# Gated graph network and graph attention in one kernel: the attention weights of the last pair but one are transposed on TensorE

## The chip, the cores and the metric

The kernel runs on one core of a Trainium2 chip. The metric is the device time of one execution in microseconds (us). The profile is of one execution on the chip. Its engines are PE (TensorE, matmuls; PEld is its weight load), DVE (VectorE), ACT (ScalarE), POOL (GpSimd) and SP (SyncE, which only issues transfers).

## The reference

There are 64 graphs of 256 nodes with 256 features, and an adjacency matrix of integers for each. Two layers follow each other, each with a layer norm and a ReLU in front and a residual behind. The first is a gated graph network of three steps, the second a graph attention layer:

```python
# layer 0: three GRU steps
A = (adj != 0)
for i in range(3):
    m = h @ weight[i]
    aggr = einsum('bst,bsd->btd', A, m)
    gi, gh = aggr @ w_ih.T + b_ih, h @ w_hh.T + b_hh
    r, z = sigmoid(i_r + h_r), sigmoid(i_z + h_z)
    n = tanh(i_n + r * h_n)
    h = (1 - z) * n + z * h
# layer 1: attention
h = x @ W.T
e = leaky_relu((h @ a_left)[:, :, None] + (h @ a_right)[:, None, :])
e = where(adj == 0, -1e9, e)
out = softmax(e) @ h
```

All is float32.

## The kernel before

The 64 graphs are taken as 32 pairs (p = 0 to 31, G = 2 graphs g to a pair). A tile is 128 partitions by 512 float32: both graphs of a pair, or one graph as two blocks of 128 rows. Matmuls that need more than one rounded product use split operands: a float32 value is split into three tiles of the rounded type float32r (helper split, L469: part "0" on ACT at L472, "1" and "d" on DVE at L473 and L475). A projection is then a "top" of several matmuls into a PSUM bank (L497), a rescaling of that bank on ACT (L511, names with "scale"), and a "rest" (L502).

One pair goes through these stages:

- Input: norm and ReLU (norm_relu, L542), hi and lo parts for the propagation, and the transposed h, called hT.
- Three GRU layers (i = 0, 1, 2). Each splits hT ("h0", "h1"), multiplies by the adjacency ("prop 0", "prop 1", L618), splits the result ("g0", "g1"), and computes for both feature blocks db = 0, 1 the gates r, nh, ni and z. The top of r is cut in two: topT (the part of h) and topF (the part of the aggregate). ACT applies tanh (L637, L647, L650) and DVE combines (u, u add, d sub, d mul, d add: L642, L645, L654, L656, L658). At the end the new h is transposed back ("back 0", "back 1"), and either split again for the next layer or added to x ("res").
- Attention: "mid" norm and ReLU, four dots with the two halves of the attention vector (L715), the row of the right dots spread over all partitions ("right"), leaky ReLU on ACT (L741), masking (L744), row maximum (L746), exponentials with their sums (L752), then the transposition of the weights ("p turn", "p copy"), the weighted sum of the nodes ("mix", L769), the projection by W ("project", L778 or L792), and the scaled result added to x ("out", L797).

The last pair (p = 31) has its own form, so that its end is short: the third layer's gates are computed for each graph apart (names "... of 0" and "... of 1"), "back" and "right" and "p turn" are transposes on TensorE, and the attention goes by row blocks (L803 to L838, names such as "last mix 1 0"). In the last two pairs (p >= 30) the projection is one plain float32 matmul group after a copy of the mix ("mix copy", L788) instead of a split.

A transposition by DMA (dma_turn, L516) is this: one DMA transpose of the float32 tile seen as 16-bit halves, two gathers of 64 partitions each, and a copy on ACT (join, L533, its instruction at L535) that puts the halves together again. For the attention weights of pairs 0 to 30 it reads as

```python
dma_turn(f"p turn {g}", pm_[g], pT, [((rs, ALL), planes(rs), slice(None))])
join(f"p copy {g}", rs, pT)
```

with pm_ the masked exponentials and pT what mix reads.

The order of all work is made by a planner (class Plan) when the program is built. Each operation has an engine, an estimated occupation and latency, the buffers that it reads and writes, and a priority worked out backward from due times. The planner places the operations one by one, at each step the one that can start first, and of those the one of lowest priority value. The table LEAD moves the priority of single operations by so many nanoseconds; a name with "late " in front is that of pair 30, with "last " of pair 31, and with neither it holds for all pairs (a prefixed operation takes both leads). Up to four pairs are in flight, so PE works on the gates of one pair while another waits for its transfers. On each engine the instructions then run strictly in the order that the planner wrote.

Of the kernel before, what the change touches and what calls it, by code (L numbers as in the profile page):

```python
# [24 lines left out]


LEAD = {
    "w load": 17000, "w d": -3000, "in 0 eps": -2000, "in 0 relu": 71000, "in 1 stats": -3000, "in 1 relu": 57000,
    "h0 0": 3000, "prop 0": 4000, "g0 0": -24000, "g0 1": -19000, "prop 1": 30000, "g1 1": 23000, "r 0 topT": 2000,
    "ni 0 topF": -18000, "u add 0": 1000, "z 0 topF": -114000, "z 0 rest": 11000, "z 0": 55000, "d add 0": -14000,  # L30
    "r 1 topT": -55000, "nh 1 rest": 5000, "ni 1 topF": -23000, "z 1 topF": -162000, "z 1 scale": -94000,
    "z 1": 51000, "d sub 1": -3000, "d add 1": -14000, "back copy 1": -43000, "mask 0": -6000,
    "mid 1 stats": -52000, "max 1": -19000, "c0 0": 12000, "late h0 d": -6000, "late prop 0": 13000,
    "late g0 0": -52000, "late r 0 topT": -7000, "late nh 0 topF": -29000, "late r 1 topT": -8000,
    "late ni 1 topF": -30000, "late tanh 1": -20000, "last A": 11000, "last in 0 stats": 9000,
    "last in 0 eps": 1000, "last prop 1": 19000, "last g1 0": 12000, "last r 0 topT": -5000,
    "last r 0 rest": -45000, "last nh 1 rest": -3000, "last lo 0": -88000, "last back 1": -80000,
    "last ni 0 of 0 topF": 18000, "last nh 1 of 0 rest": -5000, "last ni 1 of 0 topF": 19000,
    "last r 0 of 1 topF": -19000, "last nh 0 of 1 topF": -34000, "last ni 0 of 1 topF": -37000,
}  # L40


# [164 lines left out]
def tile_gated_gnn_then_gat(  # L207
# [39 lines left out]
    nc = tc.nc  # L247
    P = 128
    B, N, D = x.shape
    L = weight.shape[0]  # L250
    NB = N // P
# [5 lines left out]
    NPAIR = B // G  # L257
# [16 lines left out]
    ALL = (0, 1)  # L274
    ONE = (0,)

    def parts(b):
        return b.t[:, :GN].rearrange("p (k d) -> p k d", k=2)
# [3 lines left out]
    def pe(name, n, fn, **kw):  # L282
        return plan.op(name, "PE", n, n + 220, fn, **kw)

    def act(name, n, fn, **kw):
        plan.op(name, "ACT", n, n + 170, fn, **kw)
# [14 lines left out]
    MM, TR, PROP, PASS = 432, 109, 120, 232  # L301
    A512, V512, S512, VP256, C512 = 475, 605, 660, 392, 522
# [6 lines left out]
    ident = const.tile([P, P], F32, name="ident")  # L309
# [206 lines left out]
    def dma_turn(name, src, t, gathers):  # L516

        view = lambda q, blocks: t.t.bitcast(U16).rearrange("p (k q n) -> p q k n", q=2, n=P)[:, q, blocks, :]
        plan.op(name, "SP", 1370, 3700, lambda: nc.sync.dma_start_transpose(
            t.t.bitcast(U16).rearrange("p (c n) -> p c n", n=P), src.t.bitcast(U16)), r=[(src, ALL)], w=[(t, ALL)])

        def gather(dst, blocks):
            for q in range(2):
                nc.sync.dma_start(dst(slice(64 * q, 64 * q + 64)), view(q, blocks))

        for region, dst, blocks in gathers:
            plan.op(name + " gather", "SP", 1320, 4800 if blocks == slice(None) else 3500, lambda dst=dst, blocks=blocks: gather(dst, blocks),  # L530
                    r=[(t, ALL)], w=[region])

    def join(name, src, dst, order="b j n"):  # L533

        act(name, 1065, lambda: nc.scalar.copy(  # L535
            dst.t.bitcast(U16).rearrange("p (j n b) -> p j n b", j=2, b=2),
            src.t.bitcast(U16).rearrange(f"p ({order}) -> p j n b", j=2, b=2)), r=[(src, ALL)], w=[(dst, ALL)])

    def planes(b):
        return lambda rows: b.t[rows].bitcast(U16).rearrange("p (b k n) -> p b k n", b=2, n=P)  # L540
# [27 lines left out]
    def pair(p):  # L568
# [5 lines left out]
        A = [Buf("round") for _ in range(G)]  # L574
        h = [Buf("full") for _ in range(G)]
        hi, lo = [Buf("round") for _ in range(G)], [Buf("round") for _ in range(G)]
        for g in range(G):
            dve2("A", 340, lambda g=g: nc.vector.tensor_scalar(A[g].t, ADJ[p][g].t, 0.0, None, op0=ALU.not_equal),
                r=[(ADJ[p][g], ALL)], w=[(A[g], ONE)])
# [3 lines left out]
                r=[(h[g], ALL), (hi[g], ONE)], w=[(lo[g], ONE)])  # L583
        hT = [Buf("full") for _ in range(DB)]
        if p > 0:
            rs = [Buf("full") for _ in range(DB)]
# [5 lines left out]
        for db in range(DB if p == 0 else 0):  # L592
            pt = Buf("bank")

            def turn(db=db, pt=pt):
                for g in range(G):
                    for nb in range(NB):
                        nc.tensor.transpose(pt.t[:, (g * NB + nb) * P : (g * NB + nb + 1) * P],
                                            parts(h[g])[:, nb, ts(db, P)], ident)
# [5 lines left out]
        for i in range(L):  # L605
            last = i == L - 1
# [23 lines left out]
            for part in [(0,), (1,)] if apart else [ALL]:  # L630
                cols, of = columns(part), " of %d" % part[0] if apart else ""
                for db in range(DB):
                    plan.due = 1000.0 * SLOT * (3 * p + 2 * i) + (8000.0 * part[0] if apart else 0)
                    d = hT[db]
                    pr = gate(f"r {db}{of}", db, [("hh", hs), (i, gs)], tops, True, part=part)
                    r_, z_, u = Buf("full"), Buf("full"), Buf("full")
                    act(f"r {db}{of}", fit(575, part), lambda b=r_, k=pr, db=db, cols=cols: nc.scalar.activation(  # L637
                        b.t[:, cols], k.t[:, cols], AF.Tanh, bias=b_rz[:, db : db + 1], scale=0.5),
                        r=[(pr, ONE), ("b_rz", ONE)], w=[(r_, ONE)])
# [12 lines left out]
                        r=[(pz, ONE), ("b_rz", ONE)], w=[(z_, ONE)])  # L652
# [10 lines left out]
            if not last:  # L663
                hi, lo = [Buf("round") for _ in range(DB)], [Buf("round") for _ in range(DB)]
            for g, db in [(g, db) for g in range(G) for db in range(DB)] if apart else []:
                hn = Buf("bank")

                def back(g=g, db=db, hn=hn):
# [6 lines left out]
                    r=[(hn, ALL)], w=[(XR[g], ALL)])  # L675
            for db in range(0 if apart else DB):
                hn = Buf("full" if away else "bank")
                if away:
                    rs = Buf("full")
# [77 lines left out]
        for g in range(G if far else 0):  # L757
            sm = sms[g]
            dve("recip", 70, lambda sm=sm: nc.vector.reciprocal(sm.t[:, 8 : 8 + NB], sm.t[:, 4 : 4 + NB]),
                r=[(sm, (1,))], w=[(sm, (2,))])  # L760
            pT, pg, pv = Buf("full"), Buf("bank"), Buf("bank")
            rs = Buf("full")
            dma_turn(f"p turn {g}", pm_[g], pT, [((rs, ALL), planes(rs), slice(None))])
            join(f"p copy {g}", rs, pT)

            def mix(g=g, pT=pT, pg=pg):
                for db in range(DB):
                    for jb in range(NB):
                        nc.tensor.matmul(pg.t[:, ts(db, N)], parts(hb[g])[:, jb, ts(db, P)],  # L769
                                         pT.t.rearrange("p (i j n) -> p i j n", j=NB, n=P)[:, :, jb, :], start=(jb == 0), stop=(jb == NB - 1))  # L770

            pe(f"mix {g}", 4 * MM, mix, r=[(pT, ALL), (hb[g], ALL)], w=[(pg, ONE)])
            if p < NPAIR - 2:
                cs = split(f"c{g}", pg, True)

                def project(js, first, cs=cs, pv=pv):
                    for n, (ib, db, j) in enumerate((ib, db, j) for ib in range(NB) for db in range(DB) for j in js):
                        nc.tensor.matmul(pv.t[:, ts(ib, D)], cs[j].t[:, db * N + ib * P : db * N + (ib + 1) * P],  # L778
                                         fac["W"][:, j, db, :], start=(first and n == 0), stop=True, skip_group_check=True)

                pe(f"project {g}", 8 * PROP, lambda project=project: project((0, 1), True),
                   r=[(cs[0], ONE), (cs[1], ONE), ("facW", ((0, 0), (1, 0)))], w=[(pv, ONE)])
                act(f"project {g} scale", A512, lambda pv=pv: nc.scalar.activation(pv.t, pv.t, AF.Copy, scale=SPLIT + 1.0), w=[(pv, ONE)])
                pe(f"project {g} rest", 4 * PROP, lambda project=project: project((2,), False),
                   r=[(cs[2], ONE), ("facW", ((0, 1), (1, 1)))], w=[(pv, ONE)])
            else:
                ag = Buf("full")
                act(f"mix copy {g}", A512, lambda ag=ag, pg=pg: nc.scalar.copy(ag.t, pg.t), r=[(pg, ONE)], w=[(ag, ALL)])  # L788

                def project_whole(ag=ag, pv=pv):  # L790
                    for ib, db in [(ib, db) for ib in range(NB) for db in range(DB)]:
                        nc.tensor.matmul(pv.t[:, ts(ib, D)], ag.t[:, db * N + ib * P : db * N + (ib + 1) * P], wT[:, db, :],  # L792
                                         start=(db == 0), stop=(db == DB - 1))

                pe(f"project {g}", 4 * MM, project_whole, r=[(ag, ALL), ("wT", ALL)], w=[(pv, ONE)])
            for nb in range(NB):
                dve(f"out {g}", VP256, lambda b=XR[g], nb=nb, pv=pv, sm=sm: nc.vector.scalar_tensor_tensor(  # L797
                    parts(b)[:, nb, :], pv.t[:, ts(nb, D)], sm.t[:, 8 + nb : 9 + nb], parts(b)[:, nb, :],
                    op0=ALU.mult, op1=ALU.add), r=[(pv, ONE), (sm, (2,))], w=[(XR[g], (nb,))])
            dma("store", 256, lambda g=g, b=XR[g]: nc.sync.dma_start(rows(out, G * p + g), parts(b)), r=[(XR[g], ALL)])  # L800


        for g, ib in [(g, ib) for g in range(G) for ib in range(NB)] if not far else []:  # L803
# [7 lines left out]
                r=[row], w=[total])  # L811
# [64 lines left out]
```

## Time and profile before

| | |
|---|---|
| median of 3 runs | 2075.97 us |
| lowest and highest | 2074.25 and 2076.62 us |
| span of the profiled execution | 2066.4 us |
| granted TensorE clock, mean | 0.998 |
| PE busy | 2045.3 us, 99% |
| ACT copies of the DMA transposes (L535) | 308 of 1165 ns, 358.9 us |
| DMA transposes | 308, 3.2 us from issue to landing (median) |
| gathers of 128 KB | 492, 3.6 us from issue to landing |

The page is of one execution; times in it are from the span's start. [...] neighbours overlap in the record: the distance from one start to the next is what PE spends. A line's "idle before" names what ended the wait. The granted clock is the share of full speed that TensorE was allowed.

### The profile page before, as it was taken

Reading aid. Unit: us, or ns where it says so; the run is one execution under the profiler, and the core shown is the slowest. Engines: PE = TensorE matmul, PEld = TensorE weight load, DVE = VectorE, ACT = ScalarE, POOL = GpSimd, SP = SyncE. Lnnn points to the kernel's source line nnn. Section 1 sums busy time; section 2 is a strip of 40 time slices with the busy share of each in tenths; the row PEclk is TensorE's granted clock in tenths of the full one; section 3 lists DMA queues with packets and bytes.
Section 4 is the critical chain, followed back from the end, with each engine's and each line's share of the span. In section 5 each row is a group of like instructions: output and inputs, shape, how many; then the busy total and the mean of one; then the engine's idle time right before and its main releaser. Section 6 shows DMA issues by size and latency. Waiting matters only on the chain.

```text
span 2066.4 us, 31380 instructions
## 1 busy us (share of the span) xinstructions
PE 2045.3 (99%) x9949; PEld 1692.7 (82%) x9949; DVE 1737.0 (84%) x3888; ACT 1761.8 (85%) x3047; POOL 157.8 (8%) x198
## 2 busy tenths in 40 slices
PE   8999999999999999999999999999999999999998
PEld 6888888888887888888888888888888888788887
DVE  7788888888888888888888888888888888888877
ACT  6788898888888888888888888888888888888876
POOL 1000000000000000000000000000000000000000
PEclk9999999999999999999999999999999999999999
DMA  4257787657776667866676766777766778666632
GB/s 129 55 108 122 128 142 108 116 106 139 132 125 104 117 121 130 141 109 113 110 136 129 125 115 117 111 133 140 112 115 118 121 128 142 104 118 108 118 72 57
DMA packets 742918, 241.52 MB, mean 117 GB/s; under 512 B 666704, under 2 KB 742752, under 8 KB 742752
## 3 DMA queue, kind: packets, MB, share of 16 engines
q1 hardware_dynamic: 742720, 239.51, 65.6%
q8 instruction: 78, 1.28, 0.3%
q14 instruction: 88, 0.72, 0.1%
q10 hardware_dynamic: 32, 0.01, 0.0%
HBM read 61.09 MB, written 16.84 MB: 38 GB/s over the span
## 4 chain that ended last, share of the span: by engine, by line
PE 85%; DMA 5%; DVE 5%; ACT 3%; issue 1%; SPq 0%; ACTq 0%; DVEq 0%
PE bank L497 45%; PE bank L502 23%; PE bank L618 8%; DMA full<-full 5%; PE bank L778 4%; PE bank L769 4%; DVE round L473 1%; ACT full L535 1%; PE bank L446 1%; DVE round L475 1%; ACT full L563 1%; ACT bank L511 1%; DVE full L656 0%; DVE full L744 0%; ACT full L637 0%
## 5 line engine op out<-in xcount | busy, mean ns | idle before, releaser
L497 PE MATMUL bank<-round,fac 128*128 128x512 f32 (+1 forms) x2328 | 617.2, 393 | 0.4
L497 PE MATMUL bank<-round,fac_hh 128*128 128x512 f32 (+1 forms) x2328 | 612.4, 395 | 0.0
L497 PEld LDWEIGHTS bank<-round,fac 128*128 128x128 f32 x2328 | 433.7, 188 | 105.3 <-DVE round L473 2.0
L497 PEld LDWEIGHTS bank<-round,fac_hh 128*128 128x128 f32 x2328 | 430.6, 188 | 96.4
L511 ACT ACTIVATE bank<-bank 128x512 f32<-128x512 f32 (+1 forms) x582 | 334.6, 577 | 95.8 <-PE bank L497 88.0
L535 ACT COPY full<-full 128x1024 uint16<-128x1024 uint16 x308 | 358.9, 1165 | 31.3 <-DMA full<-full 23.6
L502 PE MATMUL bank<-round,fac 128*128 128x512 f32 (+1 forms) x1164 | 356.8, 392 | 0.2 <-ACT bank L511 0.2
L502 PE MATMUL bank<-round,fac_hh 128*128 128x512 f32 (+1 forms) x1164 | 354.1, 394 | 0.0
L475 DVE SCALAR_TENSOR_TENSOR round<-round,round 128x512 fp32r<-128x512 f32 x444 | 304.8, 688 | 8.1
L502 PEld LDWEIGHTS bank<-round,fac 128*128 128x128 f32 x1164 | 215.1, 188 | 55.4 <-ACT bank L511 6.0
L557 POOL TENSOR_TENSOR small<-small,nhalf 128x2 f32<-128x2 f32 x128 | 123.8, 975 | 1687.2 <-DVE small L555 1611.4
L502 PEld LDWEIGHTS bank<-round,fac_hh 128*128 128x128 f32 x1164 | 206.1, 188 | 44.9 <-ACT bank L511 7.4
L618 PEld LDWEIGHTS bank<-round,round 128*128 128x128 f32 x1536 | 208.6, 190 | 14.4 <-DVE round L696 0.5
L473 DVE TENSOR_TENSOR round<-bank,round 128x512 fp32r<-128x512 f32 x252 | 172.8, 686 | 56.2 <-ACT round L472 53.3
L618 PE MATMUL bank<-round,round 128*128 128x256 f32 x1536 | 215.9, 284 | 0.3 <-DVE round L696 0.3
L642 DVE SCALAR_TENSOR_TENSOR full<-full,bank 128x512 f32<-128x512 f32 (+1 forms) x194 | 131.7, 679 | 56.4 <-ACT full L637 52.0
L647 ACT ACTIVATE full<-full,vec 128x512 f32<-128x512 f32 (+1 forms) x194 | 139.4, 719 | 40.4 <-DVE full L645 20.5
L650 ACT ACTIVATE full<-bank,b_rz 128x512 f32<-128x512 f32 (+1 forms) x194 | 132.8, 684 | 45.5 <-PE bank L502 43.9
L472 ACT ACTIVATE round<-bank 128x512 fp32r<-128x512 f32 x252 | 145.9, 592 | 28.5 <-PE bank L618 26.7
L656 DVE SCALAR_TENSOR_TENSOR full<-full,full 128x512 f32<-128x512 f32 (+1 forms) x194 | 130.4, 672 | 32.3 <-ACT full L650 32.1
L473 DVE TENSOR_TENSOR round<-full,round 128x512 fp32r<-128x512 f32 x192 | 130.9, 682 | 27.5 <-ACT round L472 24.2
L645 DVE TENSOR_TENSOR full<-full,bank 128x512 f32<-128x512 f32 (+1 forms) x194 | 131.1, 676 | 24.4 <-PE bank L502 17.4
(98 smaller groups left out, 2292.8 us busy)
## 6 DMA issues: line engine op xcount, KB each, us to landing
full<-full SPq DMA_DIRECT2D x492, 128.0 KB, 3.6
x<-in_x_dram SPq DMA_DIRECT2D x64, 256.0 KB, 3.0
adj<-in_adj_dram SPq DMA_DIRECT2D x64, 256.0 KB, 4.3
full<-in_x_dram SPq DMA_DIRECT2D x64, 256.0 KB, 3.1
full<-full SPq DMA_DIRECT2D x248, 64.0 KB, 2.5
out_dram<-full SPq DMA_DIRECT2D x62, 256.0 KB, 2.5
full<-line SPq DMA_DIRECT2D x62, 128.0 KB, 3.7
full<-full SPq DMA_TRANSPOSE x308, 3.2
```

The source lines that it names most:

```text
L472: act(name + " 0", A512 if bank else C512, lambda: nc.scalar.activation(v0.t, v.t, AF.Copy, scale=BELOW), r=[(v, ALL)], w=[(v0, ONE)])
L473: (dve if bank else dve2)(name + " 1", V512, lambda: nc.vector.tensor_sub(v1.t, v.t, v0.t.bitcast(F32)), r=[(v, ALL), (v0, ONE)], w=[(v1, ...
L475: dve2(name + " d", V512, lambda: nc.vector.scalar_tensor_tensor(vd.t, v1.t.bitcast(F32), -SPLIT, v0.t.bitcast(F32), op0=ALU.mult, op1=ALU ...
L497: nc.tensor.matmul(bank.t[:, cols], f(m, j, kb), b.t[:, cols], start=(first and n == 0), stop=True, skip_group_check=True)
L502: nc.tensor.matmul(bank.t[:, cols], f(m, 2, kb), s[kb][2].t[:, cols], start=False, stop=True, skip_group_check=True)
L511: act(name + " scale", fit(575 if "nh" in name else 515, part), lambda: nc.scalar.activation(bank.t[:, cols], bank.t[:, cols], AF.Identity ...
L535: act(name, 1065, lambda: nc.scalar.copy(dst.t.bitcast(U16).rearrange("p (j n b) -> p j n b", j=2, b=2), src.t.bitcast(U16).rearrange(f"p ...
L618: nc.tensor.matmul(pa.t[:, ts(g, N)], b, parts(A[g])[:, sb, :], start=(n == 0), stop=(n == len(terms) - 1))
L642: dve(f"u {db}{of}", fit(S512, part), lambda u=u, k=ph, b=r_, cols=cols: nc.vector.scalar_tensor_tensor(u.t[:, cols], b.t[:, cols], 1.0, k ...
L645: dve(f"u add {db}{of}", fit(V512, part), lambda u=u, k=pn, cols=cols: nc.vector.tensor_add(u.t[:, cols], u.t[:, cols], k.t[:, cols]), r=[ ...
L647: act(f"tanh {db}{of}", fit(615, part), lambda u=u, en=en, cols=cols: nc.scalar.activation(u.t[:, cols], u.t[:, cols], AF.Tanh, bias=b_i[: ...
L650: act(f"z {db}{of}", fit(575, part), lambda b=z_, k=pz, db=db, cols=cols: nc.scalar.activation(b.t[:, cols], k.t[:, cols], AF.Tanh, bias=b ...
```

## The change

For the last two pairs that take this path, p >= NPAIR - 2 (of which only p = 30 comes here, since pair 31 has its own form), the attention weights are transposed by four TensorE transposes into a PSUM bank, and one ACT copy of that bank takes the place of the re-interleaving copy. It is meant to take the latency of two DMA steps out of the way to pair 30's mix, close to the end of the program. The estimates given to the planner are four transposes (4 x TR) on PE and a bank copy (A512) on ACT. Together with it the table LEAD is another: the four entries "in 0 eps", "in 1 stats", "prop 0" and "r 0 topT", which hold for all pairs, are gone, and the 24 entries of "late" and "last" give way to nine others, so that the planner's order for the last pairs is another too.

```diff
 LEAD = {
-    "w load": 17000, "w d": -3000, "in 0 eps": -2000, "in 0 relu": 71000, "in 1 stats": -3000, "in 1 relu": 57000,
-    "h0 0": 3000, "prop 0": 4000, "g0 0": -24000, "g0 1": -19000, "prop 1": 30000, "g1 1": 23000, "r 0 topT": 2000,
...
-    "mid 1 stats": -52000, "max 1": -19000, "c0 0": 12000, "late h0 d": -6000, "late prop 0": 13000,
-    "late g0 0": -52000, "late r 0 topT": -7000, "late nh 0 topF": -29000, "late r 1 topT": -8000,
-    "late ni 1 topF": -30000, "late tanh 1": -20000, "last A": 11000, "last in 0 stats": 9000,
-    "last in 0 eps": 1000, "last prop 1": 19000, "last g1 0": 12000, "last r 0 topT": -5000,
-    "last r 0 rest": -45000, "last nh 1 rest": -3000, "last lo 0": -88000, "last back 1": -80000,
-    "last ni 0 of 0 topF": 18000, "last nh 1 of 0 rest": -5000, "last ni 1 of 0 topF": 19000,
-    "last r 0 of 1 topF": -19000, "last nh 0 of 1 topF": -34000, "last ni 0 of 1 topF": -37000,
+    "w load": 17000, "w d": -3000, "in 0 relu": 71000, "in 1 relu": 57000, "h0 0": 3000, "g0 0": -24000,
+    "g0 1": -19000, "prop 1": 30000, "g1 1": 23000, "ni 0 topF": -18000, "u add 0": 1000, "z 0 topF": -114000,
...
+    "late res 1": -12000, "late project 0": 6000, "last h0 d": -12000, "last r 0 topF": -52000,
+    "last nh 1 topF": 30000, "last ni 0 of 0 topF": 43000, "last ni 1 of 0 topF": 6000,
+    "last r 1 of 1 topT": -5000, "last z 1 of 1 topF": -9000,
 }
...
             pT, pg, pv = Buf("full"), Buf("bank"), Buf("bank")
-            rs = Buf("full")
-            dma_turn(f"p turn {g}", pm_[g], pT, [((rs, ALL), planes(rs), slice(None))])
-            join(f"p copy {g}", rs, pT)
+            if p < NPAIR - 2:
+                rs = Buf("full")
+                dma_turn(f"p turn {g}", pm_[g], pT, [((rs, ALL), planes(rs), slice(None))])
+                join(f"p copy {g}", rs, pT)
+            else:
+                pt = Buf("bank")
+
+                def turn(g=g, pt=pt):
+                    for k, (ib, jb) in enumerate((ib, jb) for ib in range(NB) for jb in range(NB)):
+                        nc.tensor.transpose(pt.t[:, ts(k, P)], parts(pm_[g])[:, ib, ts(jb, P)], ident)
+
+                pe(f"p turn {g}", 4 * TR, turn, r=[(pm_[g], ALL)], w=[(pt, ONE)])
+                act(f"p copy {g}", A512, lambda pt=pt, pT=pT: nc.scalar.copy(pT.t, pt.t), r=[(pt, ONE)], w=[(pT, ALL)])
```

In the order that the planner makes of this, PE has at the end of pair 31's third layer: the gates of graph 0, "late p turn 0", "late mix 0", "late project 0", "late p turn 1", "late mix 1", "late project 1", each with gates of graph 0 or 1 between, and then the last gates of graph 1 ("last r 1 of 1", "last z 1 of 1"). Before, all gates of both graphs stood ahead of "late mix 0".

## The prediction

> **What bounds the kernel now.** I read the page's first part, then the busy time by stage over the last 120 us, then TensorE's timeline there, since both the transposes and the changed leads act on the last pairs. The first part says that TensorE (PE) is the bound of the whole:
>
> ```profile
> PE 2045.3 (99%) x9949; PEld 1692.7 (82%) x9949; DVE 1737.0 (84%) x3888; ACT 1761.8 (85%) x3047; POOL 157.8 (8%) x198
> ```
>
> So a saving on ACT or on the DMA queue counts only where PE stands still. The busy time by stage (columns: stretch, its length, busy PE, PEld, DVE, ACT, POOL, granted PE clock, DMA share, GB/s) shows where that is:
>
> ```profile
> 1950.00:2015.00 65.00, 65.00 (x313) 53.69 (x312) 48.73 (x108) 49.47 (x86) 2.47 (x3) 1.00 0.36 69
> 2015.00:2022.00 7.00, 2.90 (x15) 2.18 (x14) 6.45 (x20) 4.41 (x8) 1.50 (x2) 0.82 0.02 1
> 2022.00:2025.00 3.00, 3.00 (x16) 3.00 (x16) 2.63 (x7) 1.87 (x4) 0.00 (x0) 0.50 0.34 24
> 2025.00:2044.00 19.00, 18.66 (x149) 18.24 (x148) 13.59 (x39) 15.22 (x41) 0.92 (x1) 0.97 0.37 80
> 2044.00:2067.00 23.00, 17.37 (x96) 14.17 (x96) 13.39 (x46) 11.58 (x29) 0.69 (x1) 1.00 0.20 58
> ```
>
> Up to 2015 PE is full. Then comes a hole of some 5 us (pair 31 goes from its second GRU layer to its third), a stretch at half clock, 19 us of gates with PE full, and a tail of 23 us that is a chain of short steps. The same view at 1 us shows the clock falling 3.8 us after the last gate matmul (2015.65) and coming back 5 us after matmuls resumed (2021.3):
>
> ```profile
> 2018.00:2019.00 1.00, 0.63 (x4) 0.39 (x4) 1.00 (x7) 0.92 (x2) 0.00 (x0) 1.00 0.00 0
> 2019.00:2020.00 1.00, 0.00 (x0) 0.00 (x0) 1.00 (x4) 0.25 (x1) 0.00 (x0) 0.73 0.00 0
> 2025.00:2026.00 1.00, 1.00 (x7) 1.00 (x7) 1.00 (x7) 0.60 (x1) 0.00 (x0) 0.50 0.45 58
> 2026.00:2027.00 1.00, 1.00 (x9) 1.00 (x9) 1.00 (x3) 0.00 (x0) 0.00 (x0) 0.85 0.08 1
> ```
>
> PE's timeline (start, us, line, operation, how many):
>
> ```profile
> 2020.56 1.11 PE L685 MATMUL bank<-ident,full 128*128 128x128 f32 x4 [1.93 <-DVE full L658]
> 2021.33 3.79 PE L618 MATMUL bank<-round,round 128*128 128x256 f32 x16
> 2024.92 3.15 PE L497 MATMUL bank<-round,fac_hh 128*128 128x256 f32 x20
> ...
> 2043.37 0.50 PE L502 MATMUL bank<-round,fac 128*128 128x256 f32 x2 [0.22 <-ACT bank L511]
> 2044.44 1.99 PE L769 MATMUL bank<-full,full 128*128 128x256 f32 x8 [0.57 <-ACT full L535]
> 2046.27 0.69 PE L670 MATMUL bank<-ident,full 128*128 128x128 f32 x4
> 2047.17 1.99 PE L792 MATMUL bank<-wT,full 128*128 128x256 f32 x8 [0.20 <-ACT full L788]
> 2049.00 0.38 PE L736 MATMUL bank<-ident,small 128*128 128x128 f32 x2
> 2049.51 1.99 PE L769 MATMUL bank<-full,full 128*128 128x256 f32 x8
> 2052.18 1.99 PE L792 MATMUL bank<-wT,full 128*128 128x256 f32 x8 [0.68 <-ACT full L788]
> ...
> 2059.32 2.05 PE L823 MATMUL bank<-full,full 128*128 128x128 f32 x16 [0.24 <-ACT full L818]
> 2061.20 1.89 PE L831 MATMUL bank<-wT,full 128*128 128x256 f32 x8
> ```
>
> The last gates (L497, L502) run from 2024.92 to about 2043.9, 18.9 us. Only then come pair 30's two mixes (L769) and projections (L792), 1.83 us each: they fill PE while pair 31's graph 1 walks its chain. That chain sets the end: its last d add ends at 2046.5, and residual, normalisation, dots, softmax, mix, projection and store take 19.9 us more, to 2066.4.
>
> [...]
>
> **The change part by part.**
>
> *Removed.* For pair 30's two graphs: a DMA transpose and a two-piece gather each, and the 1.17 us copy (L535). From the SyncE timeline, graph 0's transpose is issued at 2034.39 and its copy starts at 2043.23: 9 us of latency; for graph 1, 2040.35 to 2048.30. PE computed gates meanwhile; only 0.57 us of waiting (before 2044.44) is PE's own.
>
> *Added.* Four PE transposes per graph. L685's four take 0.35 us at full clock (1985.08 to 1985.43) and 0.77 at half (2020.56 to 2021.33), so 0.7 to 1.5 us for both; I take 0.7, as gates run densely there; plus one ACT copy of a bank, 0.59 us as for L788, in place of 1.17. Two more PSUM banks for a moment.
>
> *Moved: the leads.* Orders up to pair 29 stay but for a tiny DVE operation per pair, which hides under a full PE. In pairs 30 and 31 the same gates are shuffled. The orders of the changed program are fixed when it is built, and I walk them with the durations of this profile. In the tightest place before 2015.7, pair 30's third layer, 3.2 us of PE work stand between "late prop 1" and "late r 0 topF", and ACT and DVE need 2.2 for the split between them. I find no stall above some tenths before 2015.7, and none to remove, as PE was full. The hole keeps its cause: back 0 and back 1 wait for both d adds, and nothing stands between that PE could do. On DVE, d add 0 now comes behind "mid 1 stats" (0.8 us later) and d add 1 is ahead of the four dots (1.2 us earlier); the propositions start some 0.4 us sooner. Gates start at 2024.6.
>
> *Moved: what stands ahead of the last gate.* In the changed PE order both "late mix" and both "late project", with their "p turn", stand before "last z 1 of 1 rest"; before, they stood behind all gates. Queued behind them are graph 1's gates, and the whole final chain waits for those. PE work to the end of the last gate: 18.9 + 4 x 1.83 + 0.7 + 0.3 (one back, one right) = 27.2 us. Walking the ACT and DVE orders I find the exps, p copy and mix copy just in time, so little standing. The last gate ends at 2024.6 + 27.2 = 2051.8, against 2043.9: 7.9 us later.
>
> *The tail from there.* Zero is the end of the last gate matmul; a matmul's end to ACT is 0.25 (2015.65 to 2015.90). ACT: two leaky (0.85) ahead of z, z to 1.3, tanh to 1.7; DVE: d sub 2.1, max 0 2.75, d mul 3.1, d add 3.45. "back 1 of 1" stands behind "p turn 0 0", which waits for exps: done 3.75. res 4.4, stats 5.4, eps 5.5, pow on GpSimd 0.95, shift 6.65, relu from 6.7. On DVE the dots stand behind "out 0 0" and "out 0 1", which wait for graph 0's projections: out 0 0 to 7.95, dots done 9.9. "right 1" at 9.95, and from there to the end as before (2054.45 to 2066.4), 11.95: in all 21.9. Before it was 22.5.
> Sum: 2051.8 + 21.9 = 2073.7, or 7.3 us more than 2066.4.
>
> *The clock in the tail.* PE's work that filled this tail is gone from it. Gaps between real matmuls: from the last gate to mix 0 0 about 4.2 us, and from the last projection of graph 0 to mix 1 0 about 6.6 us (right to mix is 4.87 in the trace before). Both exceed the 3.8 us after which the clock fell. The second hits the path: mix and projection of graph 1 (3.6 us) at half clock for up to 5 us cost 2.5 to 3.6; I take 2.6. The first delays out 0 0 and the dots by 2.9; [...] I leave it out of the likeliest case and keep it for the range.
> Likeliest: 7.3 + 2.6 = 9.9 us; 2075.97 + 9.9 = 2085.9.
>
> **The rivals.**
> - Slower, without clock loss: +7.3, 2083.3. [...] Against: 6.6 us is far over 3.8.
> - Slower, with both losses: 9.9 + 2.9 = 12.8, 2088.8. The first gap is longer than the one that did it before.
> - Faster: the DMA wait was the bound of the tail. The chain of waits does pass through both gathers (3.06 and 4.12 us) into mix. If graph 1's gates lost nothing, the tail would lose "mid 1 eps" behind "late out 0" (0.8) and relu behind "mix copy 1" (0.9), and the hole 0.4: with up to 1 us of idle about -3, 2073. Against: those waits order PE's late filler, not the d add at 2046.5, and the new order puts 8.3 us ahead of the last gate.
> - No change: 0.7 of transposes against 0.4 of the hole and a shorter tail, 2076. It needs that PE work ahead of the gates be hidden, and there is no idle PE to hide it in from 2025 to 2044.
>
> **How the numbers follow.** One clock loss 0.44, both 0.26, none 0.20, no change 0.04, faster 0.06. Slower by over 0.2% (4.2 us) is thus 0.90. The range: the low end is no clock loss with a walk 3 us too long (2080.5), the high end both losses with 2 us of stalls (2091).
>
> **What would show it.** In the changed profile: late mix and project (L769's and L792's successors) before the last L502; the last L502 near 2052; the hole still there at 2016 to 2021; a granted clock of about 0.5 for some of the last 15 us. A last L502 near 2044 with the mixes spread into idle PE would prove the walk wrong, and so would a tail of 18 us or less.

## The result and the profile after

| | before | after |
|---|---|---|
| median | 2075.11 us (4 runs, 2068.92 to 2076.62) | 2085.38 us (4 runs, 2084.20 to 2085.86) |
| span of the profiled execution | 2066.4 us | 2082.2 us |
| granted TensorE clock, mean | 0.998 | 0.996 |

The ratio after to before is 1.0054, with an interval of 1.0033 to 1.0075: the changed kernel is 10 to 11 us slower. The first part of the page says nothing of that; TensorE (PE) is as full as it was, and ACT has a little less to do:

```profile
PE 2053.2 (99%) x9957; PEld 1696.9 (81%) x9957; DVE 1737.2 (83%) x3888; ACT 1758.0 (84%) x3047; POOL 159.9 (8%) x198
```

The busy time by stage does. Its columns are the stretch, its length, busy PE, PEld, DVE, ACT, POOL, granted PE clock, DMA share and GB/s. The stretches are not the same work as in the table of the kernel before, since all of it comes some 6 us later here:

```profile
1950.00:2015.00 65.00, 65.00 (x313) 53.50 (x312) 48.01 (x101) 49.47 (x86) 2.19 (x2) 1.00 0.39 75
...
2025.00:2044.00 19.00, 18.20 (x125) 17.48 (x123) 13.05 (x38) 13.15 (x34) 0.06 (x1) 0.82 0.20 42
2044.00:2058.00 14.00, 13.84 (x92) 12.72 (x90) 10.51 (x34) 8.32 (x23) 0.69 (x1) 1.00 0.11 39
2058.00:2067.00 9.00, 5.88 (x30) 5.31 (x30) 5.90 (x20) 4.64 (x13) 0.69 (x1) 0.81 0.00 0
2067.00:2083.00 16.00, 7.87 (x30) 6.20 (x30) 3.95 (x13) 3.42 (x10) 0.00 (x0) 0.72 0.10 33
```

PE is still full up to 2015. The new things are below: a second full stretch up to 2058, and 25 us at the end in which PE is half idle and, when it works, partly at a low clock (0.81 and 0.72, where the kernel before had 1.00). PE's timeline (start, us, line, operation, how many) gives the causes their names:

```profile
2021.17 0.62 PE L498 MATMUL bank<-round,fac 128*128 128x512 f32 x2
2024.57 1.26 PE L681 MATMUL bank<-ident,full 128*128 128x128 f32 x8 [2.77 <-DVE full L654]
...
2030.31 4.80 PE L493 MATMUL bank<-round,fac_hh 128*128 128x256 f32 x28
...
2042.02 0.60 PE L767 MATMUL bank<-ident,full 128*128 128x128 f32 x4
...
2043.64 1.89 PE L775 MATMUL bank<-full,full 128*128 128x256 f32 x8
2045.18 0.59 PE L498 MATMUL bank<-round,fac_hh 128*128 128x256 f32 x2
...
2052.57 1.89 PE L798 MATMUL bank<-wT,full 128*128 128x256 f32 x8
...
2057.45 0.40 PE L498 MATMUL bank<-round,fac 128*128 128x256 f32 x2
2060.81 0.69 PE L821 MATMUL bank<-ident,full 128*128 128x128 f32 x2 [2.97 <-ACT full L813]
...
2062.15 2.81 PE L829 MATMUL bank<-full,full 128*128 128x128 f32 x16
...
2071.67 1.18 PE L821 MATMUL bank<-ident,full 128*128 128x128 f32 x4 [3.05 <-ACT full L813]
2072.82 3.79 PE L829 MATMUL bank<-full,full 128*128 128x128 f32 x16
```

L767 is the new transposition, L775 "late mix", L798 "late project"; L821 and L829 are the last pair's "p turn" and mix. The mixes and projections now lie between 2043.64 and 2054.1, ahead of the last gates (L498 at 2057.45), and nothing of pair 30 is left to fill the tail. The last mix, L829 at 2072.82, took 3.79 us for the same 16 matmuls that took 2.05 before.

The chain of waits (start, us, what) agrees. Pair 30's work is on it here because gates of the last graph stand behind it:

```profile
2050.04 1.75 PE bank L775 x8
2051.79 0.95 PE bank L498 x8
2052.74 1.73 PE bank L798 x8
2054.46 0.95 PE bank L493 x8
```

To compare kernels, I cut the end of each profile at three marks on PE's timeline: the start of the last pair of 512-column gate matmuls (2021.17 here), the start of pair 31's third-layer gates (2030.31), and the start of the last pair of gate matmuls (2057.45). Worked out from the timelines, in us:

```
                        last 512-column     gates to        last gates
                        gates to gates      last gates      to the end
before                       9.74             18.45           23.03
before, again                9.46             17.86           22.88
after                        9.14             27.14           24.75
after, again                 9.06             26.04           23.95
```

The first column holds the hole. In the two first profiles the gates stage grew by 8.7 and the tail by 1.7, and the hole lost 0.6: 9.8 us, which is about the difference of the medians (10.3). In the two second profiles the sum is 8.8. The profiled executions of the first pair themselves differ by 15.8; the other 6.0 lie ahead of the first mark, and the last section shows that executions of one kernel spread by as much there.

### The profile page after: what moved, and what is told of

Same layout as the page of the kernel before. It is cut to its first block, busy times and chain, and to the rows that moved or that the text cites. A ratio compares the mean times of both kernels' runs of the same rounds, so it can differ in the third digit from the quotient of the medians.

```text
span 2082.2 us, 31380 instructions
## 1 busy us (share of the span) xinstructions
PE 2053.2 (99%) x9957; PEld 1696.9 (81%) x9957; DVE 1737.2 (83%) x3888; ACT 1758.0 (84%) x3047; POOL 159.9 (8%) x198
## 3 DMA queue, kind: packets, MB, share of 16 engines
q8 instruction: 78, 1.28, 0.3%
## 4 chain that ended last, share of the span: by engine, by line
PE 82%; DMA 7%; DVE 6%; ACT 4%; issue 1%; SPq 1%; ACTq 0%; DVEq 0%
PE bank L493 43%; PE bank L498 21%; PE bank L614 7%; DMA full<-full 6%; PE bank L784 4%; PE bank L775 4%; DVE round L469 1%; ACT full L531 1%; PE bank L442 1%; DVE round L471 1%; DVE full L652 1%; DVE full L740 1%; ACT bank L507 1%; DVE small L742 1%; SPq L523 1%
## 5 line engine op out<-in xcount | busy, mean ns | idle before, releaser
L498 PE MATMUL bank<-round,fac 128*128 128x512 f32 (+1 forms) x1164 | 357.8, 392 | 0.0
L498 PE MATMUL bank<-round,fac_hh 128*128 128x512 f32 (+1 forms) x1164 | 354.9, 395 | 1.3 <-ACT bank L507 1.3
L498 PEld LDWEIGHTS bank<-round,fac 128*128 128x128 f32 x1164 | 215.0, 188 | 55.4 <-ACT bank L507 5.9
L498 PEld LDWEIGHTS bank<-round,fac_hh 128*128 128x128 f32 x1164 | 205.9, 188 | 46.8 <-ACT bank L507 9.4
L643 ACT ACTIVATE full<-full,vec 128x512 f32<-128x512 f32 (+1 forms) x194 | 139.3, 718 | 42.2 <-DVE full L641 20.8
```

Source lines behind the costliest of these rows:

```text
L498: nc.tensor.matmul(bank.t[:, cols], f(m, 2, kb), s[kb][2].t[:, cols], start=False, stop=True, skip_group_check=True)
L643: act(f"tanh {db}{of}", fit(615, part), lambda u=u, en=en, cols=cols: nc.scalar.activation(u.t[:, cols], u.t[:, cols], AF.Tanh, bias=b_i[: ...
```

## The experiments

Two theories were tried against each other. The first is the prediction's: pair 30's mixes and projections stand ahead of the last gates and delay them by their own length, and the emptied tail then loses the clock. Its rivals: the transposes themselves cost or gain something, for instance by ending a DMA wait that bounded the tail; or the new LEAD table costs by another way, in the orders of all pairs or of the tail. All ratios are to the kernel before on the same chip.

**The kernel before, again.** One execution with a profile, as the reference for the traces of that chip: 2067.39 us, with 2068.15 as the median of the 35 executions of this kernel there. Its stages are in the table above. It was also to show where the 6.0 us ahead of the first mark come from. If executions spread, it was expected there between 2015 and 2022 us; if the new order in every pair costs them, at 2015 to 2016.5. It came at 2015.20, as in the first profile (2015.18), which fits both, so it didn't decide; the runs of the last section do.

**The transposes alone, with the order kept.** The transposition moved to TensorE as in the change, the LEAD table of before, and PE, ACT, DVE and SP held to the order of before by extra edges given to the planner, which fix an order and carry no data. The two turns (the transpositions, "late p turn") go behind "last z 1 of 0 rest" and "last nh 0 of 1 topF":

```diff
+        for a, b in zip(chain, chain[1:]):
+            plan.late.append((b, a))
...
+        "30: late p turn 0: 0; 31: last r 1 of 1 rest: 0; 31: last z 0 of 1 topF: 0; "
...
+        "30: late p turn 1: 0; 31: last z 1 of 1 rest: 0; 31: last r 0 of 1 rest: 0; "
...
+        "30: late mix 0: 0; 31: last back 1 of 1: 0; 31: last back 0 of 1: 0; 30: late project 0: 0; "
```

> Pair 30's weights transposed on TensorE as in the change, but every engine keeps the order of the kernel before; the two transpositions stand among the gates of graph 1. Theory (the cost is the place of mix and project ahead of the last gates, and the clock that falls in the tail): within -1.0 to +0.7 us of before (0.9995 to 1.0003), last gate about 0.5 us later than before, no stretch of half clock after the last gate. Rival 1 (the DMA wait bounded the tail): -2 to -4 us. Rival 2 (the TensorE transposes themselves or their ACT copies cost): +4 us or more.

2068.81 us, ratio 1.0006 (0.9998 to 1.0014), a shade above the expected 1.0003, which the interval contains. PE's timeline of this run (L783 is "late mix", L506 the last gates):

```profile
2049.31 0.51 PE L506 MATMUL bank<-round,fac 128*128 128x256 f32 x2 [0.22 <-ACT bank L515]
2049.81 1.99 PE L783 MATMUL bank<-full,full 128*128 128x256 f32 x8
```

The 0.57 us that the mix waited for the DMA's copy before is gone, and the time isn't better: the gates stage is 19.11 and the tail 22.39, which is what the turns put ahead of the gates and took from the tail. So the DMA wait was a wait of filler (work of pair 30 that only fills gaps of the last chain), and the rival "faster" falls. What the change was for gains nothing here.

**The transposes with the old LEAD table, the planner free.** The code of after and the table of before:

```diff
 LEAD = {
-    "w load": 17000, "w d": -3000, "in 0 relu": 71000, "in 1 relu": 57000, "h0 0": 3000, "g0 0": -24000,
...
+    "w load": 17000, "w d": -3000, "in 0 eps": -2000, "in 0 relu": 71000, "in 1 stats": -3000, "in 1 relu": 57000,
...
```

> The TensorE transposition with the LEAD table of the kernel before, so that the planner orders freely. In the built order late mix 0, project 0, mix 1 and project 1 stand ahead of the last gates, as in the changed kernel. Theory: slower than before by 7 to 11 us. Rival (the new LEAD table is the cause): within 2 us of before.

2078.68 us, ratio 1.0052 (1.0039 to 1.0065): by its interval the whole loss may be there, without the new table. The timeline shows what after's shows: both mixes (L779) and projections (L802) ahead of the last gates, and a slow mix at the end (L833):

```profile
2038.88 1.89 PE L779 MATMUL bank<-full,full 128*128 128x256 f32 x8
...
2042.05 1.89 PE L802 MATMUL bank<-wT,full 128*128 128x256 f32 x8
...
2048.76 1.89 PE L802 MATMUL bank<-wT,full 128*128 128x256 f32 x8
...
2053.46 0.40 PE L502 MATMUL bank<-round,fac 128*128 128x256 f32 x2
...
2069.77 3.65 PE L833 MATMUL bank<-full,full 128*128 128x128 f32 x16
```

The stages are 9.74, 26.26 and 25.14. What moves the mixes is therefore the transposition. The likely reason is that in the planner's estimate the weights are ready sooner, and a planner that places what can start first pulls the mix ahead; the estimates themselves were not compared.

**The new LEAD table alone.** The code of before and the table of after:

```diff
-            if p < NPAIR - 2:
-                rs = Buf("full")
...
+            rs = Buf("full")
+            dma_turn(f"p turn {g}", pm_[g], pT, [((rs, ALL), planes(rs), slice(None))])
```

> The new LEAD table with the DMA transposition. In the built order only late mix 0 (1.8 us) stands ahead of the last two gate operations; project 0, mix 1 and project 1 stand behind. Theory: 1 to 4 us slower than before, mostly that mix. Rival (the new LEAD table is the cause): 8 us or more slower.

2070.85 us, ratio 1.0013 (1.0006 to 1.0021), 2.7 us. Here "late mix 0" stands ahead of the last two groups of gates, and the gates stage is 2.4 longer (20.81) with a hole 0.9 longer (10.64). The new table is a small part, and not all of the 2.4 is the mix. In this profile the first 20 gate matmuls took 4.18 us, where in before they took 3.15 and in before, again 2.56: the half clock of the hole reached further into them. That makes about 1.0 of the 2.4 the clock (an estimate from these lengths), which leaves about 1.4 for the mix.

**Half of it.** The first experiment's order, with "late mix 0" and "late project 0" and their copies moved ahead of the last gates:

```diff
-        "31: last ni 1 of 1 topF: 0; 31: last back 0 of 0: 0; 31: last z 1 of 1 topF: 0; "
+        "31: last ni 1 of 1 topF: 0; 31: last back 0 of 0: 0; 31: last z 1 of 1 topF: 0; 30: late mix 0: 0; "
...
-        "31: last back 1 of 0: 0; 31: last r 0 of 1 topF: 0; 31: last nh 0 of 1 topF: 0; "
...
+        "31: last back 1 of 0: 0; 30: late project 0: 0; 31: last r 0 of 1 topF: 0; "
...
```

> As the run with every order kept, but late mix 0 and late project 0 (and their ACT copies) moved ahead of the last gates; late mix 1 and late project 1 stay behind. Theory (work ahead of the last gate costs one for one): 2 x 1.83 = 3.7 us slower than the run with the order kept, so about 1.0018 to 1.0024 of before, and no half clock in the tail, since mix 1 and project 1 still fill it. Rival (only the clock in the tail costs, the place of the work is hidden): within 1 us of before.

2074.67 us, ratio 1.0033 (1.0021 to 1.0046), more than the 1.0018 to 1.0024 that was expected. The timeline shows why:

```profile
2043.26 1.99 PE L806 MATMUL bank<-wT,full 128*128 128x256 f32 x8 [0.82 <-ACT full L802]
...
2053.07 0.32 PE L740 MATMUL bank<-ident,small 128*128 128x128 f32 x1 [0.35 <-DVE full L719]
2053.23 3.52 PE L783 MATMUL bank<-full,full 128*128 128x256 f32 x8
```

The gates stage is 23.85, 4.7 more than with the order kept: 3.5 of them are the mix and projection, 0.8 a wait of PE for the mix copy, which now also holds up gates. And with half of the filler gone, the clock already fell in the tail (0.50 from 2054 to 2056): "late mix 1" (L783) took 3.52 us instead of 1.99. The size of the first part answers to the dose; the clock comes on top, earlier than expected.

**The tail kept warm.** The kernel after, with idle matmuls into a spare bank, eight behind the last gates and twelve behind "right 1". They use constants and change nothing that is stored:

```diff
+            for _ in range(count):
+                nc.tensor.matmul(b.t, fac["hh"][:, 0, 0, :P], fac["hh"][:, 0, 0, :GN], start=True, stop=True)
...
+    filler("warm a", 8, "last z 1 of 1 rest", "last p turn 0 0")
+    filler("warm b", 12, "last right 1", "last p turn 1 0")
```

> The changed kernel with two groups of idle matmuls on TensorE (8 behind the last gate, 12 behind the right dots of graph 1) that write a bank nobody reads, so that the clock stays up; all other orders as in the changed kernel. Theory (the half clock in the tail costs what its trace shows: 0.8 us in graph 0's mix and 0.7 to 2.8 us in graph 1's transposition, mix and projection): granted clock 1.0 in the last 20 us, and 2 to 4 us faster than the changed kernel, so 7 to 8 us slower than before (1.0034 to 1.0040). Rival (the chain of ACT and DVE sets the end of the tail whatever the clock): as slow as the changed kernel, about 10 us.

2073.45 us, ratio 1.0027 (1.0017 to 1.0038): against 1.0043 and 1.0054 for after itself it took back between a third and a half of the loss, somewhat more than expected. The granted clock was 1.00 from 2053 to 2074. In the timeline the two groups are L863, and the last mixes of both graphs (L833) run at their old length:

```profile
2053.20 2.00 PE L863 MATMUL bank<-fac_hh 128*128 128x512 f32 x8
...
2057.24 2.05 PE L833 MATMUL bank<-full,full 128*128 128x128 f32 x16
...
2062.28 0.67 PE L736 MATMUL bank<-ident,small 128*128 128x128 f32 x2 [1.26 <-DVE full L715]
2062.71 2.98 PE L863 MATMUL bank<-fac_hh 128*128 128x512 f32 x12
...
2066.92 2.05 PE L833 MATMUL bank<-full,full 128*128 128x128 f32 x16
```

Its tail is 21.03 against 24.75: the clock costs 3.7 us there in the first profile of after. "right" begins 9.31 after the last gates here and 10.50 in after, so 1.2 of that come from the first gap; 2.5 come from the second.

**The leads hold pair 30 back.** The kernel after with leads that make pair 30's turn, mix and projection the last choice:

```diff
+    "late p turn 0": -60000, "late mix 0": -60000, "late p turn 1": -60000, "late mix 1": -60000, "late project 1": -60000,
...
-    "late res 1": -12000, "late project 0": 6000, "last h0 d": -12000, "last r 0 topF": -52000,
+    "late res 1": -12000, "late project 0": -60000, "last h0 d": -12000, "last r 0 topF": -52000,
```

> The changed kernel with six entries of its LEAD table set to -60000 (late p turn, late mix, late project of both graphs), so that the planner itself puts both mixes and projections behind the last gates. Theory: no more than 2 us off before, so 8 us or more faster than the changed kernel. Rival (some other order of the new table costs): 5 us or more slower than before.

2074.36 us, ratio 1.0028 (1.0017 to 1.0039). This one missed. The gates stage is 19.35, as short as hoped, but the tail is 29.31. DVE's timeline and PE's show that the same fault came back one step later:

```profile
2045.63 0.43 DVE L655 SCALAR_TENSOR_TENSOR full<-full,full 128x256 f32<-128x256 f32 x1
...
2048.87 0.88 DVE L804 SCALAR_TENSOR_TENSOR full<-bank,small,full 128x256 f32<-128x256 f32 x2 [0.72 <-PE bank L799]
2049.66 0.41 DVE L670 TENSOR_TENSOR full<-full,bank 128x256 f32<-128x256 f32 x1
```

```profile
2043.49 3.62 PE L776 MATMUL bank<-full,full 128*128 128x256 f32 x16
2046.94 1.89 PE L799 MATMUL bank<-wT,full 128*128 128x256 f32 x8
2048.67 0.38 PE L667 MATMUL bank<-ident,full 128*128 128x128 f32 x2
```

The last d add (L655) ended at 2046.06, but the transposition of its result, "back 1 of 1" (L667), stands behind both mixes and a projection and ran at 2048.67; "res" (L670) then stood on DVE behind pair 30's output. The clock adds to it: it was at half from 2053.60 to 2060.43, and the first graph's mix (L830) took 3.78 us where it took 2.05 before. To have the gates first is not enough: the whole last chain has to be ahead of the filler, step by step. To that extent the rival of "another order of the tail" holds, by the same mechanism.

**After, again.** The changed kernel once more, with its profile:

> The changed kernel, unchanged, beside the next two kernels. Theory: 8 to 12 us slower than before (1.0039 to 1.0058), with half clock twice behind the last gate. If the run with the warmed tail (1.0027) saved only the 2 to 4 us that were expected of it, this one lies at 1.0037 to 1.0047; if it saved the 5 us that the first comparison suggests, at 1.0050 or more.

2080.14 us on a chip where before took 2072.16, ratio 1.0043 (1.0030 to 1.0057). Its timeline shows what is not the same from one execution to the next:

```profile
2028.11 3.51 PE L493 MATMUL bank<-round,fac_hh 128*128 128x256 f32 x28
...
2058.43 3.53 PE L829 MATMUL bank<-full,full 128*128 128x128 f32 x16
...
2069.88 3.23 PE L829 MATMUL bank<-full,full 128*128 128x128 f32 x16
```

The first 28 gate matmuls took 3.51 us, where they took 4.80 in the first profile: there the clock stayed at half until 2033.23, some 2.9 us into the gates, here it had come back (at about 2028.0) when they began. That is the 1.1 us between the gates stages (27.14 and 26.04). In the tail the first mix lost more here, and the last one less.

**The hole warmed.** Could the clock that falls in the hole itself be had back? With the order kept, ten idle matmuls stand ahead of "last back 0":

```diff
+    filler("warm c", 10, "last z 1 rest", "last back 0")
```

> As the run with every order kept, with 10 idle matmuls (2.3 us) in the hole behind pair 31's second layer, ahead of its two back transpositions. Theory: the clock stays up, the propositions and the first gates of the third layer save the 2.4 us that half clock cost in the trace of before, and the time is 1.5 to 2.5 us below before (0.9988 to 0.9993), which would be faster than both kernels. Rival (propositions and first gates wait for DVE's splits anyway): within 0.7 us of before.

2067.13 us, ratio 0.9997 (0.9989 to 1.0005). The last 512-column gates to the gates took 9.73, as before. The busy time by stage of this run shows that the clock fell all the same, at about 2022.2, 6.3 us after the first mark (3.8 in the profile with the order kept alone):

```profile
2021.00:2022.00 1.00, 0.80 (x6) 0.69 (x6) 1.00 (x3) 0.74 (x2) 0.00 (x0) 1.00 0.00 0
2022.00:2023.00 1.00, 0.69 (x4) 0.60 (x4) 0.84 (x2) 0.48 (x1) 0.00 (x0) 0.58 0.00 0
```

So the idle matmuls were split in two groups, nine ahead of "last back 0" and seven ahead of "last back 1", once with the turns on TensorE and the order kept, and once with the DMA's turns and the order of before:

```diff
+    filler("warm c", 9, "last z 1 rest", "last back 0")
+    filler("warm d", 7, "last back 0", "last back 1")
```

> As the run with the order kept and one group of idle matmuls, with two groups (9 ahead of last back 0, 7 between last back 0 and last back 1), so that no gap between real or idle matmuls is longer than 2 us. Theory: granted clock 1.0 from 2015 us to the end of the gates, propositions in 2 us instead of 3.6, and 1.5 to 2.5 us below before (0.9988 to 0.9993). Rival (propositions and first gates wait for DVE's splits): 0.9995 or more, with waits for DVE in front of the gates.

> The kernel before, with its DMA transposition and its order, and the same two groups of idle matmuls. Theory (the transposition on TensorE by itself is worth nothing): the same time as the run before this one, within 1 us. Rival (the shorter way to the mix helps once the hole is shorter): 1.5 us or more slower than that run.

2071.89 us, ratio 1.0000 (0.9992 to 1.0009), and 2070.20 us, ratio 0.9994 (0.9985 to 1.0002). These two missed what was expected of the first, 1.5 to 2.5 us below before, though an interval reaches that far. The clock did not fall in either profile before the last matmul (mean 1.000), and the 14 proposition matmuls took 1.94 us of record, as in this timeline of the first of the two:

```profile
2024.29 0.48 PE L622 MATMUL bank<-round,round 128*128 128x256 f32 x2
2025.08 1.94 PE L622 MATMUL bank<-round,round 128*128 128x256 f32 x14 [0.31 <-DVE round L700]
```

From the last 512-column gates to the gates it is 8.37 us instead of 9.74. The saving of 1.4 us is plain in both traces, and the intervals, some 1.7 us wide to each side, neither show it nor exclude it. The two medians differ by 1.7 us where at most 1 was expected, with intervals that overlap; from the first mark to the end the traces differ by 0.6, for the gates stage is 18.73 with the turns on TensorE and 17.86 without. No version was measurably faster than the kernel before.

## Why the prediction was right

*The time.* 2085.9 was predicted, 2085.4 measured. As a difference, 9.9 us were forecast; the medians differ by 10.3, and by 8.0 on the chip where after ran again. That the forecast came within 0.5 us is thus closer than the measurement repeats.

*Removed and added.* Right that the DMA's latency was no wait of the path: with the transposes alone and the order kept nothing changed that could be measured. The turns took 0.43 us each on PE (2042.02 to 2042.37 and the gate behind it 0.08 longer; 2048.52 to 2048.95), 0.86 in all against 0.7.

*Before 2015.7.* "no stall above some tenths" held: PE was busy for all 65 us from 1950 to 2015, and went on without a pause to the hole.

*The hole.* It kept its cause: back 0 and back 1 waited 2.77 us for the d add (L654). It is 0.6 us shorter, 0.3 were said.

*Ahead of the last gate.* The step that carried the forecast. 8.3 us of added work ahead of the gates were counted (27.2 less 18.9). Where the clock was full from the first gate on, the stage is 26.04 (after, again) against 17.86 (the order of before, the hole warmed with two groups): 8.2. Each mix and projection came to 1.73 (1.54 to 1.73 in starts, and the gates behind three of them 0.18 or 0.19 longer) where 1.83 was taken. That the profile of after has 27.14 is the half clock of the hole reaching 2.9 us into the gates (to 2033.23); in before it reached 1.4 us into them (to 2026.29). The sign "last L502 near 2052" held as well: the last gates began at 2057.45, and less the 6.0 us that lie ahead of the first mark that is 2051.5.

*The tail.* 21.9 were walked from the end of the last gate, 21.03 measured from the start of the last pair of matmuls with the clock full, which is 20.8 from their end: 1.1 too long. The part before "right" was the one mis-sized: 9.95 walked, 9.07 measured. The part behind was 11.95 walked, 11.7 measured.

*The clock.* The forecast of a definite loss was the weakest step, since the traces of one kernel show different losses: behind the hole the half clock lasted 6.83 us in the first profile of after (2026.41 to 2033.23) and about 3.4 in the second (2024.6 to 2028.0). The second gap cost 2.5 us against 2.6 in the first profile, but only 1.3 in the second (from "right" to the end 14.2 and 13.0 us, and 11.7 with the tail kept warm). The first was left out of the likeliest case, and that was wrong: the clock fell there too (0.51 from 2062 to 2064 in the first profile; in the second the first graph's mix took 3.53 us, where it took 2.05 before). It cost 1.2 in the first and 1.6 in the second, not 2.9, since in the first the clock was back by 2064 and only the first graph's mix ran at half. The walk too long by 1.1 and this loss of 1.2 cancelled, so the total was right partly by luck. The length of a gap, by which the prediction judged, rested on one fall in the trace of before and does not tell the cases apart; the last section has what the traces show. To count the gaps without the transposes was the author's choice: whether transposes matter for the clock was not shown (in before, PE's records in the 3.41 us ahead of the fall were 0.66 us of transposes and nothing else).

*The rivals.* "Faster" fell with the transposes alone. "No change" needed idle PE from 2025 to 2044, and the gates stage grew by all of the work. "Both losses" was right in its mechanism and too dear in its size.

Shown by experiment are the place of the mixes (old table and new turns: the whole loss; order kept: none; half of the work: 4.7 of the 8.2 us in the gates stage) and the clock of the tail (with idle matmuls the tail is 2.9 to 3.7 us shorter in the traces). Not tried is an order that has the turns on TensorE, and every step of the last chain ahead of filler, other than the one of before.

## What to carry to other kernels

PE ran its queue in order here: "back 1 of 1", whose input was ready at 2046.06 where the leads hold pair 30 back, ran at 2048.67, behind both mixes and a projection. In such a queue a piece of work that becomes ready sooner is not yet a gain: look where the planner then puts it, and count what stands behind it and who waits for that. Work of an older pair was worth most here as filler in the last chain's gaps. Taken out of there it cost twice, its own length ahead of the path (8.2 us) and the clock in the gaps that it left (3.7 us of tail in the first profile of after, against the tail kept warm).

## What the runs showed of the hardware

How long a gap between matmuls was (transposes left out, from the recorded end of one to the start of the next) does not tell whether the clock fell. It held in gaps of up to 2.0 us in the warm tail of after, and in one of 2.8 (2061.98 to 2064.82 where the leads hold pair 30 back; the clock was 1.00 from 2062 to 2070). In the run with ten idle matmuls in the hole it fell at about 2022.2, 3.4 us after the recorded end of the last of them (2018.75), although two propositions had run at 2021.61. At 3.9 to 4.3 us it fell in both profiles of after (the first graph's mix took 2.81 and 3.53 us) and in the half-moved order (3.52 us), but not in the run with the new leads alone, whose last mix came 4.2 us after the projection ahead of it and took 2.05 us, as in before.

Nor was the half clock of one length. The first profile of after, cut where the granted clock changes (it is the third number from the end):

```profile
2026.41:2033.23 6.82, 6.28 (x30) 6.08 (x29) 5.99 (x19) 2.86 (x7) 0.00 (x0) 0.50 0.14 17
2033.23:2060.54 27.31, 24.61 (x180) 23.41 (x178) 18.63 (x52) 18.65 (x49) 0.69 (x1) 1.00 0.16 45
2060.54:2063.95 3.41, 3.14 (x15) 3.13 (x16) 2.17 (x9) 1.45 (x6) 0.28 (x1) 0.50 0.00 0
2063.95:2070.78 6.83, 3.39 (x19) 2.45 (x18) 3.71 (x13) 2.57 (x6) 0.41 (x1) 1.00 0.11 38
2070.78:2077.61 6.83, 5.94 (x23) 5.17 (x24) 0.52 (x3) 2.58 (x8) 0.00 (x0) 0.50 0.00 0
```

In the profile of before the half clock lasted 6.83 us (2019.46 to 2026.29). In these two traces each of these lengths is close to 1, 2 or 8 times 3.41 us. Behind the second gap the half clock lasted 6.83 us here and reached into the last projection (L837, 2.50 us); in the other profile of after that projection took 1.89 us, and the gap cost 1.3 us instead of 2.5.

What went with the falls in these two traces is how full PE was. In lengths of 3.41 us counted from a fall, PE's records with the transposes (the ends of matmuls are modelled in them) cover 0.66 us of the length ahead of the fall in before, and 1.59, 0.72, 0.65 and 1.28 us ahead of the four falls in after (2026.41, 2060.54, 2070.78 and 2081.02). Of every other such length from 9 us on they cover at least 1.71 us. Whether it is the cause was not tried.

Where the falls lie against the work differs between executions: the clock first fell 5.2 us after the first mark in one profile of after and 5.5 in the other, and 4.3 in the first profile of before. A gap of about 4 us thus cost time in three of these profiles and none in a fourth.

Executions of one kernel spread by about as much as the change costs, and the spread comes long before the end. On one chip 35 executions of the kernel before lay between 2064.78 and 2074.41 us. Two profiles of kernels whose instructions are the same up to the hole reached the last pair of 512-column gates at 2014.96 (half ahead) and 2020.46 (order kept). The first profile of after was 6.0 us behind before at that mark, and it had come to that gradually but not evenly, with 0.6 by 165 us, 2.9 by 542, 1.2 by 795, 3.6 by 1360 and 5.7 by 1675. The new table is no likely cause: the kernel with that table alone reached the mark at 2014.81, and the one with leads that hold pair 30 back, which has the whole change, at 2014.11, while the kernel before with idle matmuls in the hole, which has none of it, came at 2021.47. Nor is it the clock, which was full from 9 us to the hole in the first profiles of before and after. What makes the spread was not tried. Two spans alone would have put the change at 15.8 us; stages cut at marks in the work gave 9.8, near the 10.3 of the medians.
